# Part of an MLP moved into the attention before it, its weights scaled on ScalarE, and a modelled order of the work up to the first scan

## The chip, the cores and the metric

The kernel runs on one core of a Trainium2 chip. The metric is the device time of one execution in microseconds. The engines are named as in the profile: PE (TensorE, matmuls), PEld (its weight loads), DVE (VectorE), ACT (ScalarE), POOL (GpSimd), SP (SyncE, which here only issues DMA transfers).

## The reference, cut to what matters

The input x is (4, 1024, 128), float32. Four layers follow, each a residual: sparse attention, an MLP with binary weights, a Mamba block, and the same MLP again.

```python
x = x + attn(_layernorm(x), Wq, Wk, Wv, Wo)        # 16 heads of 8, window 32, and every 64th key before it
x = x + ffn(_layernorm(x), k0, k1, k2, s0, s1, s2)
x = x + mamba(_layernorm(x), ...)                  # layer norm inside it, with ln_g and ln_b
x = x + ffn(_layernorm(x), k0, k1, k2, s0, s1, s2)

def _conn_dense(kernel_bool, x):                   # ffn
    w = jnp.where(kernel_bool, 1.0, -1.0)
    return x @ w
h = jnp.concatenate([x, -x], axis=-1)
h = s0 * _conn_dense(k0, h)                        # 256 -> 512
h = jax.nn.relu(h) * 2
h = s1 * _conn_dense(k1, h)                        # 512 -> 512
h = jax.nn.relu(h) * 2
h = s2 * _conn_dense(k2, h)                        # 512 -> 128

def step(h, inp):                                  # mamba: 256 channels, 16 states, over 1024 rows
    dt_t, B_t, C_t, u_t = inp
    dA = jnp.exp(dt_t[..., None] * A)
    h = dA * h + (dt_t * u_t)[..., None] * B_t[:, None, :]
    y_t = jnp.einsum('ben,bn->be', h, C_t)
    return (h, y_t)
```

## The kernel before

x stays in on-chip memory, in tiles of 128 rows, two batches (a "pair") in one array `xs[bp]`: a tile holds 64 rows of each of the two, so a pair has 16 tiles. A *chunk* is four tiles. The kernel has four stages.

**Attention** (`attention`). Its turns i = -7 to 36 are a software pipeline written out by hand: in turn i, `at(k, stage)` issues a stage of tile i + k. The program keeps this order. For each four tiles, `prep_steps(cc)` prepares queries, keys and values: normalised rows xn, their transpose xnT, projections pq, pk, pn, the keys of the window through DRAM (kT to kx) and the values too (vd to vr). It begins seven turns ahead (`LEAD`) and is taken in two steps a turn. A tile's own work: ps, the scores of the window on PE; prod, the products with the strided keys on POOL, summed on DVE; S and mx, the softmax on DVE; E, its exponential on ACT; prodv, pa, ep and eo, the two value sums, on POOL, PE, ACT and DVE; pt and po, transposes, oT, py, the output projection; `residual`, the sum into x.

**Middle.** When the attention ends, DVE makes the MLP's weights w0, w1 and w2 from the binary codes k0s, k1s and k2s (which lie in the constants from the start), and further Mamba constants are loaded (`vec` and what follows it, mostly on POOL's queue) or made (spread, w_conv). Then comes the MLP of the first pair (`early`, by chunks a0_0 to a0_3) in two *lanes*, streams of small pieces of work. A chunk is normalised and transposed (ftpa, fxnTa); its first layer is pfa, made into two fp32r halves h1a by ACT and DVE; its second layer is pga and h2a; its third is pfoa, and DVE adds it to x. With two chunks done, `mamba_norm(0, 0)` and `(0, 1)` normalise the first eight tiles, which are the first halves of both batches, for the Mamba block (statistics mv_z, factors rs_z on POOL, mxn, mxnT), and `mamba_pre_half(0, 0)` prepares the first *part*: pc (convolution and projection), u (silu), px, dtl, pd, dt, du, and B and C rows, of which B goes through DRAM (bd to bs) to all partitions. The pieces of `first` and of the lanes are taken in turn, each a piece at a time, until the first part is prepared.

**Scans.** There are eight parts, a batch b and a half f of its rows, in the order (0,0), (1,0), (0,1), (1,1), (2,0), (3,0), (2,1), (3,1), and each has 16 states: 128 *units*. (The second half of the rows begins with the state carried from the first.) In a unit ACT makes da (exp), POOL db, DVE the two scans hs and the product hc with C (spread to all partitions by PE, pcc), POOL and PE sum the states (hc, pys). Between units `pieces` takes pieces from the other works: Mamba preparation of the next parts, its norms, its output (`mamba_out`), and the lanes' MLP chunks, where `early` is the first MLP and `late` (buffers ending in b: ftpb, pfb, pgb, pfob) the second. How much is taken is set by rates per engine:

```python
    RATES = {"pe": 2.9, "ve": 1.2, "sc": 2.4, "gp": 1.2}
```

What is taken less than the rate is owed to the next units. If a part is not prepared when its first unit comes, `ready` takes pieces until it is; `hurry` in `mamba_pre_half` lets its pieces go first when the part's turn is near. Fillings may hold three PSUM banks (`SPARE`).

**Tail.** The pieces left are issued in the order of a small model of each engine's time (`issue`); then the MLP of the last batch (buffers ending in c, 256 columns at a time) ends the kernel.

Of the kernel before, what the change touches and what calls it, by code (L numbers as in the profile page):

```python
# [16 lines left out]
F32 = mybir.dt.float32  # L17
BF16 = mybir.dt.bfloat16
I32 = mybir.dt.int32
U8 = mybir.dt.uint8  # L20
# [23 lines left out]
def hybrid_kernel(ctx: ExitStack, tc: tile.TileContext, x, Wq, Wk, Wv, Wo, ln_g, ln_b, W_in, conv_w,  # L44
# [56 lines left out]
    k0s = const.tile([P, 2, FF], U8, name="k0s")  # L101
    k1s = const.tile([P, 4, FF], U8, name="k1s")
    k2s = const.tile([P, 4, C], U8, name="k2s")
    scal = const.tile([P, 4], F32, name="scal")

    def load_mlp():
        for t, k in ((k0s, k0), (k1s, k1), (k2s, k2)):
            nc.sync.dma_start(t, k.rearrange("(i p) f -> p i f", p=P))
        for i, s in enumerate((s0, s1, s2, res_scale)):
            nc.sync.dma_start(scal[:, i : i + 1], s.partition_broadcast(P))  # L110
# [88 lines left out]


    def attention(actx):
# [8 lines left out]
        pr = actx.enter_context(tc.tile_pool(name="attpr", bufs=5, space=PSUM))  # L210
# [63 lines left out]
        def prep_steps(cc):  # L274
# [3 lines left out]
            xn = ap2.tile([P, 4, C], F32, name=f"xn{cc}", tag="xn")  # L278
# [11 lines left out]
            xnT = ap2.tile([P, CH], F32, name=f"xnT{cc}", tag="xnT")  # L290
# [25 lines left out]
            if cc == 0:  # L316

                sc.copy(qT, pq)
                for t in range(4):
                    ve.tensor_tensor(  # L320
                        kx[:, t], pk[:, t * P : (t + 1) * P].unsqueeze(1).to_broadcast([P, HB, P]),
                        head_of.unsqueeze(2).to_broadcast([P, HB, P]), ALU.mult,
                    )
            else:
                kT = ap2.tile([P, CH], F32, name=f"kT{cc}", tag="kT")
                sc.copy(kT, pk)
                queues = (nc.sync, nc.gpsimd) if cc == 1 else (nc.sync,)
                for h in range(H):
                    rows = slice(h * HD, (h + 1) * HD)
                    queues[h % len(queues)].dma_start(  # L330
                        kx[rows, :, h % HB, :], kT[rows, :].rearrange("p (t x) -> p t x", t=4)
                    )
                sc.copy(qT, pq)
# [9 lines left out]
            vr = ap2.tile([P, 16, C], F32, name=f"vr{cc}", tag="vr")  # L343
# [7 lines left out]
        S, E, prods, prodv, ew, psum, outs = ({} for _ in range(7))  # L351
# [54 lines left out]
        def softmax_scores(i):  # L406
# [9 lines left out]
            mx = pw.tile([P, H], F32, name=f"mx{i}", tag="mx")  # L416
# [119 lines left out]
        def residual(i):  # L536
            bp, m = tiles[i]
            ve.tensor_add(xs[bp][:, m, :], xs[bp][:, m, :], psum.pop(("y", i))[:, :C])
# [3 lines left out]

        starts = {(3 if cc == 1 else 4 * cc) - LEAD: cc for cc in range(len(tiles) // 4)}
        preps = []
        last = len(tiles)
        for i in range(-LEAD, last + 5):
            def at(k, stage):
                if 0 <= i + k < last:
                    stage(i + k)
# [3 lines left out]
            if i == 0:  # L553
                load_mlp()
# [14 lines left out]
            if i >= 0:  # L569
                at(1, scores)  # L570
                at(1, keep_scores)
            at(0, softmax_scores)
            at(0, softmax_exp)
# [5 lines left out]
            at(-3, values)  # L579
            at(-4, keep_out)  # L580
# [7 lines left out]
            cc, step = divmod(i + 1, 4)  # L588
            if 0 <= cc < last // 4:
                spread_values(cc, range(step, step + 1))  # L590
# [60 lines left out]
    fw = ctx.enter_context(tc.tile_pool(name="ffnw", bufs=1))  # L651
    fx = ctx.enter_context(tc.tile_pool(name="ffnx", bufs=2))
    with tc.tile_pool(name="kload", bufs=1) as kl:


        sign = fw.tile([P, 2], F32, name="sign")
        below = fw.tile([P, 2], F32, name="below")
        ve.tensor_single_scalar(sign, scal[:, 0:2], 0.0, op=ALU.is_gt)
        ve.tensor_single_scalar(below, scal[:, 0:2], 0.0, op=ALU.is_lt)
        ve.tensor_sub(sign, sign, below)  # L660
        total = fw.tile([P, 1], F32, name="total")
        ve.tensor_mul(below, scal[:, 0:2], sign)
        ve.tensor_scalar_mul(below, below, 2.0)
        ve.tensor_mul(total, below[:, 0:1], below[:, 1:2])
        ve.tensor_mul(total, total, scal[:, 2:3])
        twice = fw.tile([P, 2], F32, name="twice")
        ve.tensor_scalar_mul(twice, sign, 2.0)

        w0 = fw.tile([P, FF], F32R, name="w0")
        diff = kl.tile([P, FF], F32, name="diff")  # L670
        ve.tensor_sub(diff, k0s[:, 0], k0s[:, 1])
        ve.tensor_scalar_mul(w0, diff, twice[:, 0:1])
        w1 = fw.tile([P, 4, FF], F32R, name="w1")
        ve.tensor_scalar(w1, k1s, twice[:, 1:2], sign[:, 1:2], ALU.mult, ALU.subtract)
        w2 = fw.tile([P, 4, C], F32R, name="w2")
        ve.tensor_scalar(w2, k2s, 2.0, -1.0, ALU.mult, ALU.add)
    waste = fw.tile([P, C], F32, name="waste")
    fed = set()
# [123 lines left out]
    def vec(name, src, n):  # L802
        t = mw.tile([P, n], F32, name=name)
        nc.gpsimd.dma_start(t, src.rearrange("(h p) -> p h", p=P))
        return t

    g_t, b_t = vec("ln_g", ln_g, 1), vec("ln_b", ln_b, 1)
    cb_t, bdt_t, dp_t = vec("cb", conv_b, NH), vec("bdt", b_dt, NH), vec("dp", D_param, NH)
    w_in = mw.tile([P, 2 * E], F32, name="w_in")
    nc.sync.dma_start(w_in, W_in)  # L810

    w_xp = mw.tile([P, NH, 6 * N + DR], F32, name="w_xp")
    xp = W_xp.rearrange("(h p) r -> p h r", p=P)
    for i in range(3):
        nc.gpsimd.dma_start(w_xp[:, :, 2 * N * i : 2 * N * (i + 1)], xp[:, :, DR:])
    nc.gpsimd.dma_start(w_xp[:, :, 6 * N :], xp[:, :, :DR])
    w_dt = mw.tile([6 * N + DR, E], F32, name="w_dt")
    nc.gpsimd.dma_start(w_dt[6 * N :, :], W_dt)
    a_t = mw.tile([P, NH, N], F32, name="a_t")
    nc.gpsimd.dma_start(a_t, A_log.rearrange("(h p) n -> p h n", p=P))  # L820
    sc.activation(a_t, a_t, AF.Exp)
    ve.tensor_scalar_mul(a_t, a_t, -1.0)
    w_out = mw.tile([P, NH, C], F32, name="w_out")
    nc.sync.dma_start(w_out, W_out.rearrange("(h p) c -> p h c", p=P))
    gp.tensor_scalar_mul(w_out, w_out, scal[:, 3:4])

    w_conv = mw.tile([P, DC, E], F32, name="w_conv")
    with tc.tile_pool(name="cload", bufs=1) as cl:
        taps = cl.tile([P, E, DC], F32, name="taps")
        nc.sync.dma_start(taps, conv_w.partition_broadcast(P))  # L830
        ve.tensor_mul(
            w_conv, w_in[:, :E].unsqueeze(1).to_broadcast([P, DC, E]), taps.rearrange("p e k -> p k e")
        )
# [4 lines left out]

    carry = [mw.tile([P, NH, N], F32, name=f"carry{b2}") for b2 in range(2)]

    spread = mw.tile([P, N, P], BF16, name="spread")
    minus_i = mw.tile([4 * N, 4 * N], BF16, name="minus_i")
    ve.tensor_scalar_mul(minus_i, ident[: 4 * N, : 4 * N], -1.0)
# [9 lines left out]
    def mamba_norm(bp, c):  # L853
# [9 lines left out]
        mv = yield from ln_sums(tiles, f"z{u}", soon=bp == 0)  # L863
        yield Piece(gp=2.7)

        rs = small.tile([P, 5, 4], F32, tag="rs2", name=f"rs_z{u}", bufs=2)
        gp.tensor_scalar_add(rs[:, 0], mv[:, :, 1], EPS)
        gp.tensor_scalar(rs[:, 1], mv[:, :, 1], 1.0 + EPS, EPS * EPS, ALU.mult, ALU.add)
        both = rs[:, 0:2].rearrange("p a n -> p (a n)")
        gp.tensor_tensor(both, both, minus_half, ALU.pow)  # L870
        gp.tensor_scalar_mul(rs[:, 4], mv[:, :, 0], -1.0)
        gp.tensor_mul(rs[:, 2:4], rs[:, 0:2], rs[:, 4:5].to_broadcast([P, 2, 4]))
        gp.tensor_scalar_add(rs[:, 0], rs[:, 0], 1.0)
        yield Piece()
# [385 lines left out]
    def stream(*kinds):  # L1260
        for k in kinds:
            yield from k
# [5 lines left out]
    def in_scan_buffers(u):  # L1268

        return [m2.tile([P, 2, CH], F32R, name=f"h1{u}_{f}", tag="hc", bufs=6) for f in range(4)]  # L1270

# [4 lines left out]
            early(0, lane, f1, lane, *[in_scan_buffers] * lane),  # L1276
# [9 lines left out]
    with banks(8):  # L1286
        first = [
            Work(stream(*(mamba_norm(0, c) for c in first_half))),
            Work(mamba_pre_half(*parts_in_order[0])),
        ]  # L1290
        turn = 0
        while (*parts_in_order[0], NH - 1) not in prepared:
            turn += 1
            if turn == 12:
                ve.tensor_tensor(
                    spread,
                    spread_ids[:, 0].unsqueeze(2).to_broadcast([P, N, P]),
                    spread_ids[:, 1].unsqueeze(2).to_broadcast([P, N, P]),
                    ALU.is_equal,
                )  # L1300

            wanted = first[-1].may() and "pe" in first[-1].next.us
            for w in first + ([] if wanted else lanes):
                if w.may():
                    w.run()
        for w in lanes:
            while w.next.evict or w.held:
                w.run()
    with banks(SPARE), tc.tile_pool(name="wide", bufs=1, space=PSUM) as wide:
        keep.append(True)  # L1310
        works.extend([
            first[-1],
# [49 lines left out]
```

## Time and profile before

Three runs took 911.22 us (median; 908.57 to 916.24). The profile is of another execution:

| | us |
|---|---|
| that execution's own time | 918.07 |
| its span on the core | 916.3 |
| attention, to the last residual | 247.4 |
| first scan begins | 326.79 |
| last scan ends | 876.25 |
| PE busy | 753.9 |
| DVE busy | 755.0 |
| ACT busy | 592.2 |
| POOL busy | 746.7 |
| mean granted clock of PE | 0.912 |

All times in the text are from the start of the span. Every operation is recorded on line 57, the helper that issues it, so groups are told apart by their tiles' names: `pga<-h1a,w x64` is 64 matmuls that make pga of h1a and a weight tile. "PE 18.61 of 20" is its busy time in a stretch of 20 us. A matmul's record can overlap the next one's, so a burst's length is taken from the chain of waits or from the busy time, not from the mean.

### The profile page before, as it was taken

Reading aid. Unit: us, or ns where it says so; the run is one execution under the profiler, and the core shown is the slowest. Engines: PE = TensorE matmul, PEld = TensorE weight load, DVE = VectorE, ACT = ScalarE, POOL = GpSimd, SP = SyncE. Lnnn points to the kernel's source line nnn. Section 1 sums busy time; section 2 is a strip of 40 time slices with the busy share of each in tenths; the row PEclk is TensorE's granted clock in tenths of the full one; section 3 lists DMA queues with packets and bytes.
Section 4 is the critical chain, followed back from the end, with each engine's and each line's share of the span. In section 5 each row is a group of like instructions: output and inputs, shape, how many; then the busy total and the mean of one; then the engine's idle time right before and its main releaser. Section 6 shows DMA issues by size and latency. Waiting matters only on the chain.

```text
span 916.3 us, 15271 instructions
## 1 busy us (share of the span) xinstructions
PE 753.9 (82%) x5642; PEld 453.7 (50%) x5642; DVE 755.0 (82%) x1014; ACT 592.2 (65%) x1299; POOL 746.7 (81%) x580
## 2 busy tenths in 40 slices
PE   5888668875688969898889789868989789869977
PEld 2455435543466545443445445424545356535657
DVE  6699898999643258899888999998999999999952
ACT  4775537753345577798786887887777865655432
POOL 6699996999533087899989999999998999898720
PEclk9799969997588979799998999979999989979999
DMA  4633123330010021122111111111121211122100
GB/s 125 127 72 71 43 35 69 73 67 2 28 21 1 14 80 69 48 69 70 47 71 46 68 63 57 69 66 51 70 82 46 81 70 70 58 80 70 35 11 24
DMA packets 47162, 53.09 MB, mean 58 GB/s; under 512 B 4824, under 2 KB 38400, under 8 KB 47088
## 3 DMA queue, kind: packets, MB, share of 16 engines
q1 hardware_dynamic: 45920, 51.59, 19.6%
q8 instruction: 44, 0.72, 0.3%
q0 software_dynamic: 608, 0.27, 0.2%
q10 hardware_dynamic: 560, 0.26, 0.1%
q14 instruction: 30, 0.25, 0.1%
HBM read 45.82 MB, written 4.46 MB: 55 GB/s over the span
## 4 chain that ended last, share of the span: by engine, by line
DVE 30%; PE 25%; POOL 21%; ACT 13%; issue 8%; DMA 2%; SPq 0%; DVEq 0%; POOLq 0%; ACTq 0%
DVE hs L57 15%; POOL db L57 6%; PE pga L57 5%; DVE hc L57 4%; POOL prod L57 4%; POOL prodv L57 3%; POOL hc L57 3%; ACT da L57 3%; DVE S L57 3%; PE pys L57 3%; ACT L57 3%; PE pgb L57 2%; PE pgc L57 2%; POOL ep L57 2%; PE pfoa L57 1%
## 5 line engine op out<-in xcount | busy, mean ns | idle before, releaser
L57 POOL TENSOR_TENSOR db<-du,bs 128x1024 f32<-128x1024 f32 x128 | 303.9, 2375 | 0.5 <-DMA bs<-bd 0.5
L57 ACT ACTIVATE da<-dt,a_t 128x512 f32<-128x512 f32 x256 | 175.1, 687 | 113.2 <-DVE hs L57 112.6
L57 POOL TENSOR_TENSOR hc<-hc,hc 128x512 f32<-128x512 f32 x128 | 163.9, 1281 | 36.4 <-DVE hc L57 36.0
L57 DVE TENSOR_TENSOR hc<-hs,pcc 128x1024 f32<-128x1024 f32 x128 | 155.7, 1217 | 31.3 <-PE pcc L57 24.3
L57 DVE TENSOR_TENSOR_SCAN hs<-da,db 128x512 f32<-128x512 f32 x128 | 149.6, 1207 | 15.6 <-ACT da L57 14.7
L57 DVE TENSOR_TENSOR_SCAN hs<-da,carry,db 128x512 f32<-128x512 f32 x128 | 157.0, 1267 | 2.9 <-ACT da L57 0.8
L57 PE MATMUL pys<-hc,ident 128*128 128x512 f32 x256 | 142.4, 641 | 2.1 <-POOL hc L57 2.1
L57 PE MATMUL pga<-h1a,w 128*128 128x512 f32 x256 | 78.6, 462 | 7.4 <-ACT gate L57 4.1
L57 PE MATMUL pcc<-bc,spread 96*128 96x512 bf16 x128 | 51.2, 400 | 32.2 <-DVE hc L57 31.1
L57 PEld LDWEIGHTS pys<-hc,ident 128*128 128x128 f32 x256 | 48.9, 203 | 54.8 <-issue 29.8
L57 POOL TENSOR_TENSOR prodv<-vS,E 128x128 f32<-128x128 f32 (+14 forms) x30 | 69.6, 2321 | 5.5 <-ACT E L57 5.2
L57 POOL TENSOR_TENSOR prod<-kv,qs 128x128 f32<-128x128 f32 (+14 forms) x30 | 71.2, 2374 | 1.5 <-DVE or L57 1.4
L57 PEld LDWEIGHTS pga<-h1a,w 128*128 128x128 f32 x256 | 54.5, 216 | 30.0 <-ACT gate L57 5.4
L57 ACT ACT_TABLE_LOAD x48 | 61.6, 1283 | 3.5 <-issue 2.6
L57 PE MATMUL pgb<-h1b,w 128*128 128x512 f32 x192 | 59.3, 453 | 2.3 <-DVE h1b L57 2.3
L57 PE MATMUL pc<-mxnT,w_conv 128*128 128x512 f32 x128 | 60.2, 596 | 1.0 <-ACT gate L57 1.0
L57 ACT ACTIVATE E<-S 128x512 f32<-128x512 f32 (+15 forms) x62 | 26.5, 472 | 52.2 <-DVE S L57 52.0
L57 PE MATMUL ps<-kx,qT 64*32 64x256 f32 x1008 | 46.7, 437 | 5.7 <-DVE S L57 4.7
L57 PEld LDWEIGHTS pgb<-h1b,w 128*128 128x128 f32 x192 | 38.0, 200 | 25.8 <-issue 9.7
L57 PE MATMUL py<-woT,oT 128*128 128x128 f32 x64 | 17.7, 363 | 39.6 <-ACT oT L57 39.3
L57 POOL TENSOR_TENSOR ep<-ep,eo 128x512 f32<-128x512 f32 x32 | 41.2, 1289 | 9.9 <-ACT ep L57 8.7
L57 ACT COPY ep<-pt 128x512 f32<-128x512 f32 x32 | 18.8, 587 | 38.4 <-DVE eo L57 35.9
(223 smaller groups left out, 1549.3 us busy)
## 6 DMA issues: line engine op xcount, KB each, us to landing
bs<-bd SPq DMA_DIRECT2D x64, 512.0 KB
vr<-vd SPq DMA_DIRECT2D x32, 256.0 KB
vd<-kv SPq DMA_DIRECT2D x8, 256.0 KB
x<-in_L_attn_a_x_dram SPq DMA_DIRECT2D x15, 128.0 KB
kx<-kT SPq DMA_DIRECT2D x104, 16.0 KB
out_dram<-x SPq DMA_DIRECT2D x12, 128.0 KB
taps<-in_L_attn_b_conv_w_dram SPq DMA_DIRECT2D x1, 512.0 KB
k1s<-in_L_ffn_k_dram SPq DMA_DIRECT2D x1, 256.0 KB
```

The lines of the kernel that those rows point to most:

```text
L57: ins = getattr(self.engine, name)(*args, **kwargs)
```

## The change

1. The MLP of the first eight tiles of pair 0 (chunks a0_0 and a0_1) is issued in turns 17 to 33 of the attention, while the second pair's tiles are worked on. It goes by pairs of tiles (256 columns), four PE steps a pair, one step a turn (`first_te`), after `values`; what ACT and DVE do with a step's result comes a turn later, at the start of ACT's turn (`first_sc`) and before `softmax_scores` (`first_ve`).
2. The MLP's weights are made in turns 16 to 19. The codes are loaded in turn 15 into the room of the first pair's keys and values. ACT, not DVE, scales w0 and w1.
3. Most of the Mamba constants are loaded on SP's queue in the attention (`load_mamba` in turn 8, `finish_mamba` in turn 14). w_conv and spread are made in a work of their own in the middle (`tables_between`).
4. To make room in the attention: the softmax maxima lie in an unused part of an earlier py bank, and the spare banks go from 5 to 6; xn, xnT, kT and vr have one buffer instead of two; vr's loads come two turns later; the second preparation starts one turn later; `spread_values` takes two heads in each of two turns instead of one in each of four.
5. The statistics of the eight tiles for their MLP are taken in turns 15 and 16, those of the first four for the Mamba norm in turn 33, and its factors too (`ready_factors`).
6. In the middle, the lanes begin with a0_2 and a0_3, and the pieces are chosen by a small model (`free`, `since`): the piece that can start first goes next, lanes with 1 us of handicap. The program keeps the order so found.

The diff, cut to its core:

```diff
+    def norm_factors(u, mv):
+        rs = small.tile([P, 5, 4], F32, tag="rs2", name=f"rs_z{u}", bufs=2)
...
+    def mlp_weights(k0s, k1s, k2s):
...
+        ve.tensor_sub(w0, k0s[:, 0], k0s[:, 1])
+        sc.activation(w0, w0.bitcast(F32), AF.Identity, scale=twice[:, 0:1])
+        ve.tensor_scalar(w2, k2s, 2.0, -1.0, ALU.mult, ALU.add)
+        for i in range(2):
+            yield
+            part = slice(2 * i, 2 * i + 2)
+            sc.activation(w1[:, part], k1s[:, part], AF.Identity, bias=sign[:, 1:2], scale=twice[:, 1:2])
...
-        pr = actx.enter_context(tc.tile_pool(name="attpr", bufs=5, space=PSUM))
+        pr = actx.enter_context(tc.tile_pool(name="attpr", bufs=6, space=PSUM))
...
-            mx = pw.tile([P, H], F32, name=f"mx{i}", tag="mx")
+            mx = (left_over.pop(i) if i in left_over else spare(f"mx{i}"))[:, C : C + H]
...
+        def first_te(k):
+            p, step = divmod(k, 4)
+            h1, xnT, h2, xn = (first[n] for n in ("h1", "xnT", "h2", "xn"))
+            if step == 0:
+                if p:
+                    po = first["po"] = spare(f"mo{k}")[:, :cols]
+                    for t in range(2):
+                        for f in range(4):
+                            te.matmul(po[:, t * C : (t + 1) * C], h2[:, f, t * C : (t + 1) * C], w2[:, f].bitcast(F32), ...)
+                if 2 * p < FIRST:
+                    tp = first["tp"] = spare(f"mt{k}")[:, :cols]
+                    for t in range(2):
+                        te.transpose(tp[:, t * C : (t + 1) * C], xn[:, t * C : (t + 1) * C], ident)
+            elif step == 1:
...
+                            te.matmul(pf[:, f], w0[:, (f0 + f) * P : (f0 + f + 1) * P], xnT[:, s], ...)
+            else:
...
+                            te.matmul(pg[:, f], w1[:, j, (f0 + f) * P : (f0 + f + 1) * P], h1[:, j, s], ...)
...
+            if 0 < step <= STEPS:
+                first_sc(step - 1)
             at(-1, strided_products)
...
+            if 0 < step <= STEPS:
+                first_ve(step - 1)
+            if NT <= i < NT + 4:
+                next(weights_made, None)
             at(0, softmax_scores)
...
             at(-3, values)
+            if 0 <= step < STEPS:
+                first_te(step)
             at(-4, keep_out)
...
-            early(0, lane, f1, lane, *[in_scan_buffers] * lane),
             early(0, 2 + lane, f1, lane),
             early(1, lane, f1, lane),
...
     with banks(8):
+        keep.append(True)
         first = [
+            Work(mamba_pre_half(*parts_in_order[0])),
             Work(stream(*(mamba_norm(0, c) for c in first_half))),
-            Work(mamba_pre_half(*parts_in_order[0])),
+            Work(tables_between()),
         ]
...
         while (*parts_in_order[0], NH - 1) not in prepared:
...
-            wanted = first[-1].may() and "pe" in first[-1].next.us
-            for w in first + ([] if wanted else lanes):
-                if w.may():
-                    w.run()
+            able = []
+            for w in first + lanes:
+                if not w.may() or (w in lanes and w.next.banks and w.held + w.next.banks + sum(v.held for v in first) > 5):
+                    blocked.add(w)
+                    continue
+                if w in blocked:
+                    blocked.discard(w)
+                    since[w] = max(since[w], end)
+                start = max([since[w], *(free[k] for k in w.next.us)])
+                able.append((start + (1.0 if w in lanes else 0.0), len(able), start, w))
+            start, w = min(able)[2:]
+            us = w.next.us
+            w.run()
```

## The prediction

> **What bounds the kernel now.** I read the slices first, for the stages; then busy time by stretches; then, stage by stage, the chain and the waits.
>
> ```profile
> PE   5888668875688969898889789868989789869977
> DVE  6699898999643258899888999998999999999952
> POOL 6699996999533087899989999999998999898720
> PEclk9799969997588979799998999979999989979999
> ```
>
> A slice is 22.9 us. There are four stages. The attention lasts to 247 us (last residual sum at 247.41). A middle follows, in which DVE falls to 2 tenths and POOL to 0, up to the first scan at 326.79. The 128 scan units (one state over half of one batch's rows; the last scan ends at 876.25) keep DVE and POOL at 9. A tail of 40 us has almost only PE. Their sizes: 247 + 80 + 549 + 40 = 916.3.
>
> ```profile
> core 0: us, PE busy (x) PEld busy (x) DVE busy (x) ACT busy (x) POOL busy (x), PEclk, DMA share, GB/s
> 160.00:180.00 20.00, 18.61 (x403) 11.83 (x393) 19.27 (x38) 16.20 (x43) 18.98 (x15) 1.00 0.40 80
> 220.00:240.00 20.00, 10.83 (x285) 8.44 (x283) 16.89 (x22) 4.55 (x11) 19.55 (x8) 0.65 0.01 2
> 240.00:260.00 20.00, 14.05 (x108) 9.28 (x99) 14.07 (x31) 10.67 (x26) 10.59 (x15) 0.60 0.22 54
> 260.00:280.00 20.00, 20.00 (x106) 16.87 (x105) 3.26 (x6) 6.96 (x13) 0.86 (x2) 0.97 0.00 1
> 880.00:900.00 20.00, 18.48 (x108) 13.96 (x107) 5.18 (x16) 5.04 (x11) 1.49 (x3) 1.00 0.02 8
> ```
>
> Two halves of the second pair's attention differ. At 160 to 180 us PE has 1.4 us free of 20, DVE 0.7: nothing fits in for nothing. At 220 to 240 PE has 9.2 free and POOL 0.45: there matmuls are hidden. At 260 to 280 and in the tail PE alone is full, so each matmul removed there counts whole.
>
> ```profile
> 260.45 15.32 PE pga L57 x64
> 275.77 5.37 PE pfoa L57 x48
> 301.30 6.87 PE pc L57 x16
> 309.08 3.57 PE pfoa L57 x32
> 318.58 5.49 PE pga L57 x16
> 326.79 2.35 DVE hs L57 x2
> ```
>
> These lines of the chain of waits (start, length) say that MLP matmuls set the middle's length; the Mamba work proper is pc and the short links between.
>
> **The change part by part.** Prices come from the profiled execution (918.07 us, span 916.3), which is 6.9 above the median of the runs, 911.22; I work out the difference on the first and apply it to the second. The changed order of instructions does what it says: the 8 tiles' MLP matmuls stand in turns 17 to 33 of the attention.
>
> *Middle.* Two of the four MLP chunks of the first pair leave it, and the matmuls of the others no longer stand ahead of the Mamba work. What is left runs from the last output copy (246.5). Residual 0.9; twelve statistics on DVE, of which the last four are for the Mamba norm, 12 x 0.44 = 5.3; its factors on POOL 2.7 (before: 283.88 to 286.64); hand-overs 0.6: +9.5. Four normalisations (0.43 each), 1.7, transposes and copies, 2.4: +13.6. Then pc 7.0, silu 0.7, px 1.9, a copy of B and C 0.6, the way of B through DRAM to all partitions 5.6 (from the copy's end at 317.15 to db's start at 322.76), db 2.35: 31.8, so the first scan at +32. The clock of PE is 0.60 before this burst and 0.97 when it is busy; the burst of pc at the lower clock would be 7.0 x 0.97/0.60 = 11.3, so 0 to +4.3; I take +3, nearer the cold row, because PE is idle before pc. So 35 against 80.3: **-45** (-50 to -41). The Trainium skill ("TensorE: Matmul & The Clock Gate", "What's actually happening") states that the slow state lasts some 3.4 us of sustained work at half clock; by that the burst would lose an estimated 1.7, and the sum be 1.3 lower.
>
> Constants that were loaded on POOL's queue (12 issues, 250.7 to 258.7) go to SP's early: POOL waits there for mv_z anyway (23.0 in the waits), so nothing is won. On SP, where an issue for kx takes 0.78, they put off what is queued behind them by some 9, a turn or two, and that is for a preparation seven turns ahead: 0, at most +5, within the attention's bounds.
>
> *Attention.* Each pair of tiles adds PE steps in four turns: 2 transposes and 8 matmuls of the pair before (8 x 0.228 + 0.4 = 2.2), 8 matmuls of 256 columns (8 x 0.118 = 0.95; 64 took 7.57), 16 (1.9) and 16 (1.9): 7.0 a pair, 28 in all. A PE-bound turn costs 4.85 already. Turn 19: 4.85 + 1.9 = 6.8 against 4.4, +2.4. Turn 20: 6.8 against 5.5, +1.3. Turns 21 and 22: +1.3, where ACT's loop (7.4 with the new normalisations, copies and scaling) stands close. Turns 23 and 24: +1.0. From turn 26 the period is 7.4 to 9, set by POOL:
>
> ```profile
> 203.72 2.69 POOL prodv L57
> 206.68 3.77 POOL prod L57
> 210.44 1.23 POOL ep L57
> ```
>
> PE's 5.2 + 1.9 fits, so the later pairs cost 0; if POOL's cover went, they would cost up to 14. Further, eight statistics (0.44 each), nine tiny operations and the weights on DVE in turns 15 to 17: +2.5. ACT in turn 17: +2.0. Four statistics on DVE after the last pair: +2.0. Statistics that leave the first pair: -1.5. The attention's buffers go from two to one, with preparation a turn later and the value rows two turns later: the first turns would feel this, and there DMA and DVE waits of 1.8 and 6.0 stand at 28 to 31 us, so -2 to +2, I take 0. The row maxima share the bank of a py whose sum was read five turns before: no instruction more, 0. Values are spread for two heads in each of two turns instead of one in four: the work is the same, and what it adds to ACT in turn 21 is in the +1.3. Sum **+11**, bounds 0 (all hidden) to +28 (no matmul hidden).
>
> The scaling of w1 and w0 goes from DVE to ACT:
>
> ```profile
> L57 DVE TENSOR_SCALAR w<-k1s,twice,sign 128x2048 fp32r<-128x2048 uint8 x1 | 1.3, 1339 | 0.0
> L57 ACT ACTIVATE h2c<-pgc 128x256 f32<-128x256 f32 x8 | 3.0, 384 | 3.9 <-PE pgc L57 3.9
> L57 ACT ACTIVATE h2c<-pgc 128x512 f32<-128x512 f32 x4 | 2.4, 588 | 1.5 <-PE pgc L57 1.5
> ```
>
> 256 columns more cost ACT 0.2, so w1 takes 2 x (0.59 + 0.41) = 2.0 and w0 0.6: 2.6 on ACT for 1.34 + 0.48 = 1.8 on DVE; this is in the +2.0 of turn 17 and its neighbours. The rule in the Trainium skill ("ScalarE: Activation LUTs", "Rules for kernel authors") speaks against this part: it gives multiplications to VectorE rather than ScalarE. By it the sum would fall by 0.8; by the rows of these turns the difference is moot, DVE having 0.7 of 20 free and ACT 3.8.
>
> *Scan.* The two lanes that carry the remaining MLP chunks enter it about one chunk behind: before, chunk a0_2 and half of a0_3 were done at the first scan; now only the first layer of a0_2. Counting the program's instructions between first and last scan: DVE has 4 statistics, 4 hidden-layer operations, 2 residuals and 3 normalisation operations fewer: 4 x 0.44 + 4 x 0.68 + 2 x 0.75 + 3 x 0.64 = 7.9; PE about 17.6 fewer. DVE needs 462 for the scans' own work (149.6 + 157.0 + 155.7 in the groups) and some 60 for the fillings; about 27 are stalls.
>
> ```profile
> PE pcc L57 <- DVE hc L57: 31.1, 37, 2.5
> DVE hc L57 <- PE pcc L57: 24.3, 19, 3.7
> ```
>
> Such stalls are what the change makes more of. Fillings are given out at fixed rates per unit, and a part not yet prepared when its turn comes is prepared at once, ahead of all else. Before, pc to du of the third batch's first half stand at units 45 to 56 and the part starts at 64; changed, at 60 to 63. Its second half: 74 to 88 before, 92 to 95 changed, start 96. From the end of unit 59's product, PE then has 0.4 + 1.9 + 1.0 + 7.0 queued, ACT silu 0.7, px 1.7, copies 0.6 and 0.6, and pcc 0.5 behind them: 14.4, where DVE would be ready for pcc at 6.1: unit 61 stalls 8.3, with da of unit 62 behind silu on ACT and two table loads (1.28 each). Units 60 to 63 take some 27 against 14.7: +12; units 92 to 95 some 31 against 16: +15; the second part (31 against 25 for its du, start 32) +3. Less the 8 on DVE and 4 of stalls now there: **+18** (-12 if no burst shows, +35 if each burst brings cold PE and late DMA too).
>
> *Tail.* What the scan did not take is issued after the last unit. There the changed order has 72 more second-layer matmuls, 20 first-layer, 48 output matmuls and 12 transposes: 72 x 0.235 + 20 x 0.235 + 48 x 0.228 + 12 x 0.15 = 34. PE is 18.48 of 20 busy there, so all of it counts, with little more for gaps: **+35** (+30 to +40).
>
> Sum: 11 - 45 + 18 + 35 = **+19**: 937 against the profiled 918, and 930 against the median.
>
> **The rivals.** *The scan absorbs the late preparation* (the other side): PE has some 65 us idle in the scan and ACT and PE wait for DVE (the waits above), so the bursts at units 60 and 92 hide behind DVE. Then the scan gives -12 instead of +18: 11 - 45 - 12 + 35 = -11, 900. It decides once the three delays (30 together) cost under 11: there the sum is 0. For it: before, preparation ran beside the scans at little cost. Against: pcc of the very next units is queued behind it. *A draw*: attention +6, bursts half (scan +4), tail +33: -2, about 909 to 912. Nothing speaks for it but the errors. *The moved MLP isn't hidden*: POOL's turns grow with PE's and ACT's (both py and ep wait on oT and eo in the trace), so all 28 land: 28 - 45 + 18 + 35 = +36, 947; with the scan's upper end, 964. Against: PE's 9.2 free of 20 at 220 to 240. That the change doesn't do as it says is excluded by the order of its instructions.
>
> **How the numbers follow.** Forecast (slower, own range 921 to 946) 0.49; scan absorbs 0.21; draw 0.16; not hidden 0.14. A measurement of this kernel tells about 1% (9.1 us) from no change, by the spread of the runs. So faster 0.21, same 0.16, slower 0.63. The range reaches down to the absorbing rival with the attention's lower bound, 11 less (889), and up to 954, between the forecast's own end (946) and the worst rival's (964).
>
> **What would show it right or wrong.** The last residual at 258 (247.4 + 11), turns 19 and 20 near 6.8 us, later turns as before; the first scan at 293 (258 + 35); a scan of 567; gaps of 8 us on DVE's product at units 61 and 93; last scan's end to the end 75. It is wrong if the attention is 25 longer, if scan units 60 to 63 take under 18 us, or if the tail is under 60.

## The result, and the profile after

The changed kernel took 959.06 us (median of four runs, 958.31 to 960.53) against 913.73 for the kernel before on the same chip: a ratio of 1.050, 95% interval 1.045 to 1.056. It is 45 us slower; the forecast was 930, and its range ended at 954. The profiled execution took 958.31 us with a span of 956.5, 40.2 longer than the one before. The slices of the page (each 23.9 us now) show where:

```profile
PE   5887668988757987879997698996668899888898
DVE  6699797799954889898999865989981999997332
POOL 6799955689864879999899986889993899985100
PEclk9899678999857989798997697998677999899899
```

The valley of DVE after the attention is narrower (5 and 4, where there were 4, 3, 2 and 5). But two new valleys stand in the scans (DVE 8 6 5 and 8 1, with PEclk at 7 in the deepest slice of each), and the tail covers the last three slices (3 3 2) instead of not quite two (5 2).

By stages, from the last residual of the attention, the first scan and the end of the last product of DVE (differences of the profiled executions):

| us | attention | middle | scans | of these, units 60 to 63 and 92 to 95 | tail | span |
|---|---|---|---|---|---|---|
| before | 247.7 | 79.1 | 550.8 | 16.3 and 17.7 | 38.7 | 916.3 |
| changed | 267.9 | 37.4 | 572.6 | 30.9 and 37.9 | 78.7 | 956.5 |
| difference | +20.2 | -41.7 | +21.8 | +14.6 and +20.2 | +40.0 | +40.2 |
| forecast | +11 | -45 | +18 | +12 and +15 | +35 | +19 |

The late preparation is there. DVE's timeline at units 92 to 94 (start, length, operation; in brackets the idle time before it and what ended it):

```profile
715.61 2.33 DVE L57 TENSOR_TENSOR_SCAN hs<-da,db 128x512 f32<-128x512 f32 x2
731.81 1.22 DVE L57 TENSOR_TENSOR hc<-hs,pcc 128x1024 f32<-128x1024 f32 x1 [13.88 <-PE pcc L57]
741.39 1.22 DVE L57 TENSOR_TENSOR hc<-hs,pcc 128x1024 f32<-128x1024 f32 x1 [5.92 <-PE pcc L57]
```

and the chain of waits in the same stretch names what PE did before the two pcc that DVE waits for: pc, px and pd of the part that starts at unit 96, and pz, for gates:

```profile
716.48 3.78 PE pz L57 x4
720.27 7.07 PE pc L57 x16
727.34 1.90 PE px L57 x4
...
733.96 3.44 PE pd L57 x4
737.41 3.71 PE pz L57 x4
```

In the waits between first and last scan the line of this wait grew from 24.3 us (19 times, longest 3.7) to

```profile
DVE hc L57 <- PE pcc L57: 45.7, 12, 13.9
```

### The profile page after: what moved, and what is told of

The parts are those of the page before. It is cut to its first block, busy times and chain, and to the rows that moved or that the text cites. A ratio compares the mean times of both kernels' runs of the same rounds, so it can differ in the third digit from the quotient of the medians.

```text
span 956.5 us, 15457 instructions
## 1 busy us (share of the span) xinstructions
PE 782.3 (82%) x5722; PEld 462.9 (48%) x5722; DVE 762.9 (80%) x1017; ACT 595.3 (62%) x1302; POOL 743.3 (78%) x565
## 4 chain that ended last, share of the span: by engine, by line
DVE 36%; PE 25%; POOL 21%; ACT 10%; issue 7%; DMA 1%; DVEq 0%; POOLq 0%; ACTq 0%
DVE hs L57 13%; POOL db L57 9%; DVE S L57 6%; POOL hc L57 5%; PE pc L57 4%; DVE hc L57 4%; DVE or L57 3%; PE pys L57 3%; POOL rs_z L57 2%; ACT da L57 2%; DVE py L57 2%; ACT L57 2%; PE pgb L57 2%; PE pga L57 2%; PE pgc L57 2%
## 5 line engine op out<-in xcount | busy, mean ns | idle before, releaser
L57 PE MATMUL pys<-hc,ident 128*128 128x512 f32 x256 | 153.3, 685 | 10.6 <-POOL hc L57 10.5
L57 PE MATMUL pcc<-bc,spread 96*128 96x512 bf16 x128 | 54.5, 426 | 47.3 <-DVE hc L57 45.4
L57 PEld LDWEIGHTS pys<-hc,ident 128*128 128x128 f32 x256 | 51.7, 218 | 74.8 <-POOL hc L57 33.8
L57 PE MATMUL pgb<-h1b,w 128*128 128x512 f32 x192 | 56.2, 441 | 4.0 <-ACT h2b L57 2.1
L57 PE MATMUL ps<-kx,qT 64*32 64x256 f32 x1008 | 46.3, 438 | 15.3 <-DVE S L57 12.8
L57 PE MATMUL pga<-h1a,w 128*128 128x512 f32 x192 | 56.4, 439 | 1.8 <-ACT gate L57 1.6
L57 POOL TENSOR_TENSOR ep<-ep,eo 128x512 f32<-128x512 f32 x32 | 41.0, 1280 | 18.3 <-ACT ep L57 17.7
L57 PEld LDWEIGHTS pga<-h1a,w 128*128 128x128 f32 x192 | 37.6, 198 | 20.4 <-issue 7.0
L57 PEld LDWEIGHTS pc<-mxnT,w_conv 128*128 128x128 f32 x128 | 25.0, 196 | 32.9 <-issue 32.2
L57 PE MATMUL py<-woT,oT 128*128 128x128 f32 x64 | 15.6, 328 | 29.7 <-ACT oT L57 16.7
```

The costliest lines, as they stand in the source:

```text
L57: ins = getattr(self.engine, name)(*args, **kwargs)
```

## The experiments

Each kernel is the changed one but for the edit shown, unless it says otherwise. Stages come from each run's own profile; ratios are to the kernel before on the same chip.

**More PE time for fillings.**

```diff
-    RATES = {"pe": 2.9, "ve": 1.2, "sc": 2.4, "gp": 1.2}
+    RATES = {"pe": 3.2, "ve": 1.2, "sc": 2.4, "gp": 1.2}
```

> The changed kernel with one number altered: fillings may take PE 3.2 us a unit instead of 2.9. In the order of instructions the last-minute convolution of the third batch's first half moves from unit 60 to 55-56, that of its second half from 92 to 83-84, and the MLP matmuls after the last unit fall from 69.5 us worth to 42.2. Theory (the scan's fillings run one chunk late, so parts are prepared at the last minute and MLP work is left for the tail): units 60-63 and 92-95 fall from 30.9 and 37.9 us to 16 to 22 each, the tail from 79 to 52, the rest of the scan grows by 5 to 15; total -40 to -55, near 910. Rival (PE's total work and clock set the time of scan and tail together, and the tail's 27 us come back as scan): total -15 to 0, 944 to 959.

930.11 us, ratio 1.019 (1.012 to 1.025). Tail 45.9, units 92 to 95 15.5, but units 60 to 63 still 31.3, and the scans as a whole 576.6, 4 longer. So 33 us of the tail came into the scans and cost 26 there beside the bursts (576.6 - 31.3 - 15.5 = 529.8, against 572.6 - 30.9 - 37.9 = 503.8 of the changed kernel): MLP work in the scans is not free, as neither theory had it in full. What the run won is one burst (22 us) and 7 of the tail. The other burst was expected to go: pc of that part had moved to units 55 to 57, as expected, but its pd still came in unit 62, and there DVE waits 12.8 us for a pcc behind the statistics of a later norm on ACT and then pga, pd and pz on PE. So pc at the last minute is not the only thing that makes a burst.

**The same number in the kernel before.**

> The kernel before with the same altered number, PE 3.2 us a unit. Theory (there the fillings are in time already, so the number has nothing to mend; 5 us more MLP work is left for the tail): within 1% of the kernel before, 905 to 922. Rival (the higher rate is simply better, whatever the kernel): 10 us or more faster, so that it would say nothing of the change.

920.05 us, ratio 1.010 (1.006 to 1.014): no help, slightly slower, with scans of 555.1 and a tail of 42.0, as the theory had it. The rate mends something that only the changed kernel has.

**The MLP a turn later in the attention.**

```diff
-            step = i - NT - 1
+            step = i - NT - 2
```

> The changed kernel with all MLP steps in the attention one turn later (turns 18 to 34). Theory (in turn 17 ACT's queue stands behind the first normalisation, which waits 5.4 us for factors that POOL has not made yet, and DVE then 3.5 us for its result): both waits go, the attention ends 4 to 7 us earlier, the total falls by as much; nothing else moves. Rival (the turns are as long as the work in them, whatever waits): 0 to -1.

960.24 us. The two waits in turns 17 and 18 went, and up to the last tile's turn the run was 2.5 us ahead, counted from the same start (its first pair began 2.8 later). The last turns, where the MLP's last steps now stand, gave that back: the attention ended at 270.4, no earlier. The total is the rival's.

**The attention without the MLP.** The calls of `first_norm`, `first_te`, `first_sc` and `first_ve` are left out.

> The changed kernel without the MLP of the first eight tiles (its normalisation, matmuls, copies and sums are left out, so these tiles go on as the attention left them); weights, statistics, loads and buffers stay as changed. Theory (the MLP steps cost the attention 12 to 15 us, the statistics and weights 5 to 8, the smaller buffers nothing): the attention ends at 252 to 256 instead of 267.9. Rival (single buffers, later preparation and shared banks cost most of the 20 us): it ends at 262 or later.

The attention ended at 258.7; its first pair began 2 us later than in the changed kernel's run, so the MLP steps cost 11 of the 20 and the rest of the edits 9. The theory had 12 to 15 for the MLP and 5 to 8 for the others, so both lie just outside it, and the end lies between theory and rival. Single buffers and later preparation cost nothing in the turns up to 13: there the run stays within 0.2 us of the kernel with the order alone (below), counted from the same start. The start is another matter: the first residual comes at 50.3 to 53.1 us in the thirteen profiles with the changed attention, of which the changed kernel's own is the earliest, and at 49.0 to 50.8 in the three with the old one, some 2 us later on average.

**Half of an engine's part.** First DVE's low half of the hidden layer, then half of the second layer's matmuls:

```diff
-                    ve.scalar_tensor_tensor(
-                        h1[:, :, 1], first["pf"][q], 0.0, h1[:, :, 0].bitcast(F32), ALU.max, ALU.subtract
-                    )
...
-                                pg[:, f], w1[:, j, (f0 + f) * P : (f0 + f + 1) * P], h1[:, j, s],
+                                pg[:, f], w1[:, j, (f0 + f) * P : (f0 + f + 1) * P], h1[:, j, 0],
```

> The changed kernel without DVE's part of the hidden layer in the attention (the low half of h1m is not made; PE multiplies the high half twice, so its work is the same). DVE loses 8 operations of 0.65 us in turns 19 to 32. Theory (DVE, not PE or POOL, sets the turns that the MLP lengthens): the attention ends 4 to 7 us earlier, near 262. Rival (PE's steps set them): within 1.5 of 267.9.

> The changed kernel with half of the second layer's matmuls in the attention (only the high half of h1m is multiplied): PE loses 8 x 0.118 = 0.95 us in each of eight turns, 7.6 in all; DVE's and ACT's work is the same. Theory (PE sets only turns 19 to 21): the attention ends 1 to 3 us earlier. Rival (PE's steps set the lengthened turns): 5 to 8 earlier.

Counted from the same start (their first residuals came 2.5 and 2.7 later), the attention ended 2.9 and 2.0 us earlier, in one run each: DVE's 5.2 us of work was worth 2.9, less than the theory and more than the rival, and PE's 7.6 was worth 2.0, as the theory had it. Where they were won differs. PE's share, 1.6, shows by the residual of turn 21 and then stays the same to turn 35: PE sets turns 19 and 20 and no later ones. DVE's is nothing up to turn 23 and about 1 us with each of the later steps in turns 23, 27 and 31. In turns 19 and 20 PE is full, as forecast; the chain of waits of the changed kernel has nothing but PE there:

```profile
171.40 2.10 PE mg L57 x16
173.50 0.44 PE pt L57 x4
173.94 0.22 PE py L57 x2
174.16 1.07 PE ps L57 x32
175.23 1.49 PE pn L57 x4
```

but from 186 to 191 us it goes through ACT's copies and DVE's h1m. The engine that sets a turn changes from turn to turn, and what is taken from one engine uncovers the next.

**The middle held until a third chunk is done**, and until a fourth is:

```diff
-        while (*parts_in_order[0], NH - 1) not in prepared:
+        while (*parts_in_order[0], NH - 1) not in prepared or ("a", 0, 2) not in fed:
```

> The changed kernel, in which the middle goes on until the third MLP chunk (a0_2) is done, so that the lanes enter the scan one chunk further on. In the order of instructions the convolution of the third batch's halves moves from units 60 and 92 to 50-51 and 79-81, and the MLP matmuls left for the tail from 69.5 us worth to 36.7. Theory (the lanes' lag makes the two bursts and the long tail): middle 37 to 50-58, units 60-63 and 92-95 from 31 and 38 to 16-22 each, scan 545-560, tail 79 to 39-44; total 915 to 930. Rival (the bursts come from the changed order or buffers of the scan itself): bursts stay near 31 and 38 and only the tail falls; 940 to 950.

> The same, but the middle goes on until both further chunks (a0_2 and a0_3) are done: the convolutions stand at 41-42 and 73-75, 34.2 us worth of MLP matmuls is left for the tail. Theory: middle 60 to 68, no bursts (16 each), scan 543-555, tail 37-41; total 915 to 930: what the middle takes, the scan and the tail give back at about one for one, so it lands beside the run with one chunk. Rival (fillings in the scan are nearly free): 8 to 15 us slower than with one chunk.

With one chunk 901.51 us, ratio 0.986 (0.984 to 0.989): faster than the kernel before. Middle 51.1, bursts gone (15.4 and 16.0), scans 538.7, tail 39.6. So 13.7 us spent in the middle saved 33.9 in the scans and 39.1 in the tail: the lanes' lag makes both losses, as the prediction had it. (It came out below the expected 915 to 930.) With two chunks 928.89, ratio 1.015 (1.012 to 1.018): the middle 20.3 longer again, the scans 9.3 longer too. The expectation that this would be given back one for one was wrong, and the rival's 8 to 15 us too small: it is 27 slower. Why the scans grew, with fewer fillings left in them, is open.

**The modelled order alone, in the kernel before.** Only the loop of the middle is the new one, with spread in a work of its own; attention and MLP are as before.

> The kernel before with one part of the change alone: the middle's pieces are chosen by the new model of order; attention, MLP in the middle and all else are the old ones. Its order of instructions from the first scan on has the convolutions at units 60 and 92 and 69.5 us worth of MLP matmuls after the last unit, as in the changed kernel. Theory (the modelled order, not the move, makes the lanes lag, and with them bursts and tail): attention 247, middle 60-70, scan 568-577 with bursts of 31 and 38, tail 77-80; total 955 to 972, as slow as the whole change. Rival (the lag matters little where the MLP was not moved): within 15 of 911.

979.47 us, ratio 1.070 (1.066 to 1.073). Scans 573.5 with bursts of 30.9 and 37.9, tail 79.2: from the first scan on its order of instructions is that of the changed kernel on all four engines, and so is its time (652.7 against 651.3). The middle took 81.1, no less than the old order's 79.1. The attention ended at 241.3, 6.4 earlier than before: the statistics and factors of the first MLP chunks, which the old order lets float into turns 5 to 20, stay out of it (1.3 of this is an earlier start). Nothing else differs in the two attentions' order on DVE, ACT and POOL.

**The move alone.** The changed kernel with the old rule in the middle:

```diff
+            wanted = first[0].may() and "pe" in first[0].next.us
+            for w in [first[2], first[1], first[0]] + ([] if wanted else lanes):
+                if w.may():
+                    w.run()
```

> The changed kernel with the old rule in the middle (each work and lane a piece in turn, lanes held back while the first part's matmuls can be issued); the move of the MLP and all else are as changed. Convolutions at units 47-49 and 77-78, 42.2 us worth of MLP matmuls for the tail. Theory: attention 268-270, middle 45-58, no bursts (15-18), scan 545-557, tail 43-47; total 903 to 927. Rival (the move itself is what costs): 935 or more.

898.44 us, ratio 0.982 (0.979 to 0.985). Attention 269.5, middle 39.0, scans 541.8, tail 45.9, bursts of 15.6 and 15.0. In spans, the move alone is worth -20.1, the order alone +58.8, both together +40.2: they add to within 2 us.

The windows of the middle say how little the new order won. Busy time of the engines and the granted clock in the changed kernel's middle,

```profile
268.00:288.00 20.00, 12.11 (x26) 5.88 (x27) 9.84 (x29) 12.87 (x29) 11.77 (x18) 0.52 0.11 33
288.00:305.00 17.00, 13.43 (x26) 5.49 (x26) 4.63 (x7) 10.63 (x16) 4.63 (x3) 0.77 0.18 64
```

and in that of the kernel with the old rule:

```profile
270.00:290.00 20.00, 17.34 (x47) 9.63 (x47) 8.42 (x9) 15.60 (x34) 6.16 (x7) 0.74 0.10 33
290.00:308.00 18.00, 16.46 (x78) 11.49 (x77) 5.48 (x8) 10.72 (x17) 5.30 (x4) 1.00 0.16 61
```

(columns: stretch, its length, PE, PEld, DVE, ACT, POOL busy with counts, granted clock, DMA). The old rule put 32 pga, 8 more pfa and 32 pfoa records, 16 us of matmuls, into PE's gaps, and the first scan came 1.6 us later. The gaps were nearly free, and with them filled the granted clock was higher and the sixteen pc took 7.2 instead of 8.5.

**Weights scaled by DVE**, on the kernel with the middle held for one chunk:

```diff
-            sc.activation(w1[:, part], k1s[:, part], AF.Identity, bias=sign[:, 1:2], scale=twice[:, 1:2])
+            ve.tensor_scalar(w1[:, part], k1s[:, part], twice[:, 1:2], sign[:, 1:2], ALU.mult, ALU.add)
```

> The changed kernel with the middle held until chunk a0_2 is done (901.5 in its run), and the MLP's weights w0 and w1 scaled by DVE instead of ACT. By the profile ACT loses 2.6 us and DVE gains 1.8 in turns 16 to 19, where ACT is busy 18.4 of 20 and DVE 14.2 at 150 to 170. Theory (there ACT's queue is the fuller one): the attention ends 0 to 2.5 earlier. Rival (DVE sets these turns): 1 to 2 later.

906.52 us, ratio 0.990 (0.987 to 0.993), 5 more than its base. The attention is 1.7 longer after turn 19 and 1.4 at its end, as the rival had it: scaling by ACT is right here, against the rule weighed in the prediction. The other part, 6.9 us in the scans at the same order of instructions, is not explained; PE took 8.5 us more for the same matmuls there.

**Lighter turns 14 and 16**, on the same base: nine tiny operations go from `ve` to `gp`, and a_t is negated by POOL in turn 15.

```diff
     def finish_mamba():
         sc.activation(a_t, a_t, AF.Exp)
-        ve.tensor_scalar_mul(a_t, a_t, -1.0)
+
+    def negate_mamba():
+        gp.tensor_scalar_mul(a_t, a_t, -1.0)
```

> The changed kernel with the middle held until chunk a0_2 is done, the nine tiny operations of the weights' scales moved from DVE to POOL in turn 16, and the negation of a_t moved from DVE in turn 14 (where it waited 4.8 us for ACT) to POOL a turn later. Theory (turns 14 and 16 lengthen by what DVE gets there, 1.3 and 4.0 us measured): the attention ends 2.5 to 4 earlier, 265 to 266.5, total 896 to 899. Rival (POOL then sets the turn): no gain or 1 to 3 later.

893.28 us, ratio 0.976 (0.973 to 0.979): the fastest of all. The attention ended at 262.0, 7.0 earlier (0.6 of it from its start), more than expected. In the changed kernel DVE's timeline has in turn 14

```profile
111.78 1.08 DVE L57 TENSOR_SCALAR a_t<-a_t 128x32 f32<-128x32 f32 x1 [4.83 <-ACT a_t L57]
```

an operation of 32 columns that waits 4.8 us, because ACT makes a_t behind its copies of the turn; the attention's next mask copy stands behind it. That is gone, worth 4.9 us at turn 15, and the tiny operations 1.6 more by turn 17.

**Both together**, the old rule in the middle and the lighter turns; then ACT's part of an MLP step behind the attention's own copies (`first_sc` placed just ahead of `first_ve`):

> The move of the MLP with the old rule in the middle (898.4 in its run), together with the lighter turns 14 and 16 (nine tiny operations and the negation of a_t on POOL). Theory (the two parts have nothing to do with each other, so their gains add: 17 from the order, 7 from the turns): attention 262, middle 39, scan 542, tail 46; 888 to 893. Rival (an earlier end of the attention is given back in the middle, where PE or the tables set the pace): 896 to 900.

> The same as the kernel with both, but ACT's part of an MLP step stands behind the attention's own copies of the turn (ep and S) instead of ahead of them. Theory (the price of the moved MLP, 12.8 us, is made by ACT's queue: the copies that POOL, PE and DVE wait for stand behind the MLP's): the attention ends 3 to 7 us earlier. Rival (the turns' PE, ACT and DVE sums take turns as the longest, so no order helps): within 1.5; or later, since DVE's part then waits for ACT in the middle of its softmax.

896.63 us, ratio 0.982 (0.979 to 0.985), and 903.55, ratio 0.989 (0.986 to 0.992). The first gains 4 in the attention, not 7 (265.3), and loses 3 of it in the tail, at the same order of instructions: the gains do not add in full. The total is the rival's, but not its reason, since the middle is as long as without the lighter turns (39.0). In turn 17 ACT now waits 7.5 us for the factors from POOL. In the run with the lighter turns alone it waits 5.4, with the same tiny operations on POOL; what has come in between them and the factors is rs_fa (139.43 to 141.26), the factors of a later MLP chunk, which the old rule lets float into turn 16. The second lengthens the attention by 10.7 (1.2 of it at the start), as the rival's last case had it: the theory that the MLP's price is the place of ACT's part is refuted, and DVE then waits 5.7 us for ACT's h1m, instead of 1.1, and 8.7 for its xnTm, instead of 4.5.

## Why the prediction was wrong

The signs of all four stages, the two bursts with their units, the mechanism and the likeliest outcome (slower) were right. The size was not: +19 forecast, +40 in the profile and +45 by the runs. Every term erred to the same side: the attention by 9 us, the tail by 5, the scans by 4, the middle by 3. The other 5 are of the base: the profiled execution of the kernel before was 4.3 above its median, that of the changed one 0.8 below. The step that failed is the attention's term.

*Attention, +11, measured +20.* The main error. "PE's 5.2 + 1.9 fits, so the later pairs cost 0": against the kernel without the MLP, from the same start, they cost 3.3 from turn 26 to turn 31, of which 1.5 came back after it. "Turns 21 and 22: +1.3. Turns 23 and 24: +1.0": 4.6 in all, since ACT's normalisations, copies and the spreading of values fall on the turns where DVE waits for h1m, as the chain above shows. From turn 19 on the sum priced almost only PE's work, and after turn 20 PE no longer sets the turn. And a term was missing: a_t's exponential and negation (`finish_mamba`) have no price in the sum, but they are a wait of DVE for ACT in the middle of a turn, 4.8 (4.9 won by taking it out). What leaves the first pair was put at -1.5; by the run with the order alone it is -5.1, which hid that wait in the difference of the two kernels. Between turns 15 and 21, where statistics, tiny operations and weights are added, the kernel without the MLP lost 7.5 against the one with the order alone; the sum had 2.5 for it and a part of ACT's 2.0.

*Middle, -45, measured -42.* The chain that was summed is the one that runs, but one link was missing. In the chain of waits of the changed kernel

```profile
271.33 0.20 POOL rs_fa L57
...
273.35 2.02 POOL rs_fa L57
275.45 2.20 POOL rs_z L57
...
280.18 0.50 ACT mxn L57
...
284.19 8.53 PE pc L57 x16
...
305.26 2.35 DVE hs L57 x2
```

POOL makes the factors of both MLP chunks (from 269.58) ahead of those of the Mamba norm, and two of its operations last ten times as long as their like, beside the tables that DVE makes at that moment (`tables_between`):

```profile
273.32 1.98 DVE L57 TENSOR_TENSOR w_conv<-w_in,taps 128x1024 f32<-128x1024 f32 x1 [0.68 <-POOL rs_fa L57]
275.21 2.30 DVE L57 TENSOR_TENSOR spread<-spread_ids 128x2048 bf16<-128x2048 int32 x1
```

So the normalisation began 13.5 after the last output copy and not 9.5; the two long operations are 3.8 of these 4.0. With the middle held for one chunk the same pair of tables stands beside the same two operations (2.00 and 2.20); no run moved the tables by themselves. The rest was nearly as summed. The cold clock was rightly allowed for, though at +3 too dearly: pc took 8.5 at a granted 0.52 to 0.77, +1.5, where 7.0 was the warm row and 11.3 the bound.

*Scans, +18, measured +22*, and *tail, +35, measured +40*: the burst at 60 was 2.6 and that at 92 5.2 dearer than worked out (the gate's pz, 3.78 and 3.71 at 92 and 3.71 at 60, stand in PE's queue too, which the sum left out). Outside the bursts the scans were 13.0 shorter, where the sum had 9 (12 by the count of instructions and stalls, less 3 for the second part). In the tail the matmuls counted were there: PE was busy 68.3 us, 35 more than before; the rest is waits between them.

*The rivals.* "The scan absorbs the late preparation" fell: units 60 to 63 and 92 to 95 cost 35 us. "The moved MLP isn't hidden", 947 to 964, named the range in which the result fell, but for the wrong reason: 11 of the MLP's 28 us showed, not 28.

*What the prediction didn't ask* is which edit makes the lag. It took the change as one: the MLP moves, so the lanes stand elsewhere. The order alone is 59 us slower, the move alone 20 faster. The argument about lanes and fillings was right for the order and charged to the whole.

Open are what sets the turns in the rest of the MLP's 11 us, beyond the 2.0 of PE and 2.9 of DVE, and the 6.9 us of the scans in the run with DVE's weights.

## What to carry to other kernels

An order of work that brings the first of a long stage's inputs soonest is not yet a good one: count what it leaves undone at that moment, and what the later stage must then do at the last minute or after its end. Here the new order won 1.6 us and lost 62. Idle gaps of an engine on a chain of dependences were here the cheapest place for work of no haste, the more so on PE, where the clock was higher with them filled; and a two-part change should be priced part by part, since a good half can hide in a bad whole.

## What the runs showed of the hardware

PE's clock followed its gaps: 0.52 granted in the changed middle, where PE was busy 12.1 of 20 us, 0.74 and 1.00 with the gaps filled. The Trainium skill ("TensorE: Matmul & The Clock Gate", "Why this matters for your kernels") advises against gaps of more than some 3 us between bursts of matmuls; the two middles agree with it, as far as two go: the longest gap is 3.2 us in the changed one, 2.3 with the old rule.

A tiny operation of DVE can be held up beside one of POOL's on which it does not depend. In turn 16 one of the nine, on 128x2 elements, shows 1.27 us where its neighbours take 0.16:

```profile
138.28 1.27 DVE L57 TENSOR_SCALAR below<-below 128x2 f32<-128x2 f32 x1
138.26 1.26 POOL L57 TENSOR_TENSOR ep<-ep,eo 128x512 f32<-128x512 f32 x1 [3.72 <-ACT ep L57]
```

It begins 0.02 after POOL's ep and ends 0.03 after it. The Trainium skill ("Trainium Architecture — The Big Picture", "What this means for kernel authors") states that DVE and GpSimd share a port pair under an exclusive lock; these two rows fit that, and so does a_t above, 1.08 us for 32 columns beside an ep that runs from 111.55 to 112.82. It goes the other way round too: rs_fa and rs_z in the changed middle, 2.02 and 2.20 us on 128x4 elements where their like took 0.20 and 0.23, end 0.07 and 0.14 after DVE's w_conv and spread. No run here took the lock away by itself.
